# Graph sums in two one-hot steps: fixed spans of chunks first, then placed into fixed blocks

## The chip, the cores and the metric

The kernel runs on one core of a Trainium2 chip. The engines are named as in the profile: PE is TensorE (matmuls; PEld its weight loads), DVE is VectorE, ACT is ScalarE, POOL is GpSimd, and SP is SyncE, which here only issues DMAs. Times are device microseconds of one execution. The figure to be predicted is the median over several executions of the changed kernel; before the change it is 2722.78 us.

## The reference

Two graph convolutions (Chebyshev, two terms) on N = 6250 nodes with 512 features, E = 100000 edges that come sorted by their target `dst`, everything in float32:

```python
h = jnp.maximum(_layernorm(x), 0.0)
norm = -dinv[src] * dinv[dst]                 # dinv from the out-degree of each node
def prop(h):
    return segment_sum(h[src] * norm[:, None], dst, num_segments=N)
h = h @ W1_0 + prop(h) @ W1_1 + b1            # first layer
h = layer_norm(h, gamma, beta)
h = where(h >= 0, h, 0.01 * h)
out = x + h @ W2_0 + prop(h) @ W2_1 + b2      # second layer
```

For each node, `prop` adds up the rows of its incoming edges, some 16 of them. The factor `dinv[src]` is in the table from which rows are read (`tab`), the factor `-dinv[dst]` is applied to the sum.

## The kernel before, in words

**Edges and gathers.** The edges are cut into 782 chunks of 128. For each chunk POOL issues one indirect DMA (L400) that gathers the 128 source rows, 256 KB, into one of 57 places of a ring in SBUF. That makes 1564 gathers for both layers; the first 16 are issued in the prologue (L246). `gather_to` issues them up to a chunk number, and a place is free again when PE has read it.

**Sums.** A block is 128 nodes in a row, four quarters of 32. `block_plan` (L37) lays 53 blocks over a layer's nodes without looking at the data: each begins at the target of an edge whose number is fixed, so the first node of a block is known only at run time. It also says, for each quarter, which chunks may hold an edge of it, with a margin for the spread (`ranges`). `sums` makes one-hot matrices on DVE: `plain` and `node` (L503, L504) are the node numbers, `sel` (L507) compares the targets `dl` with them. In layer 0, `held` (L511) counts how many edges have been found, by which the kernel knows at the end whether any was missed. The matmuls of L517 then add up the rows: `sel` of 32 columns is the weights, the 128x512 rows of a chunk are moving, and the four quarters lie in four strips of 32 columns of the array, which work side by side. A block has six or seven such steps of up to four matmuls. ACT copies the result out of PSUM as `agg` (L520), scaled by `-dinv`.

**Products.** `transposed` (L460) turns a 128x512 tile by four PE transposes. For the own part, `h` of the block goes through it to `hT`, copied out by ACT (L488), and `start_products` (L495) multiplies it with `w0`. For the sums, `agg` goes through it, DVE copies it out as `aT` (L603), and L609 multiplies it with `w1` into the same bank `u_ps`. `finish` adds the bias; in layer 0 it does the layer norm and writes the rows of the next table and of `h_tab`, in layer 1 it adds `x` and writes `out`.

**Rows at an address in a register.** Since a block begins at a node known only at run time, all that belongs to its rows is addressed by a register of SP: `load` (L464 to L480) loads the first nodes of eight blocks into registers, then the rows of `x`, the scales of each row (`sb`, 4 bytes apiece) and, in layer 1, the rows of `h_tab`. The stores in `finish` (L529, L546, L550) go the same way.

**Order.** On PE, POOL and SP the order is that of the code (`manual_schedule`); on DVE and ACT the scheduler sets it. For block b the order on PE is: transposes of block b+1's own rows, the sums of b, half of b+1's own products, the transposes of `agg`, the other half, then the products of `aT`. The gathers up to the first chunk of b plus 57 are issued on POOL when block b begins; they come after the sums of the block before, whose places they take. In layer 0 `another` (four times a block, until 60 chunks are done) scales rows that were gathered from `x` before the first table was written.

Of the kernel before, what the change touches and what calls it, by code (L numbers as in the profile page):

```python
# [19 lines left out]
P = 128  # L20
# [5 lines left out]
NQ = P // Q  # L26
RE = 16
RAW = 60
SPREAD = 3.2
# [5 lines left out]


def block_plan(N, E):  # L37

    NC = -(-E // P)
    deg = E / N

    def sd(n):
        return math.sqrt(E * (n / N) * (1 - n / N))

    n = math.ceil((E - deg * P) / (deg * P - SPREAD * sd(P)))
    step = 16 * math.ceil((E - deg * P) / (16 * n))
    over = deg + SPREAD * math.sqrt(deg)  # L50
    res = []
    for b in range(n):
        first = b * step
        end = first + step + over if b < n - 1 else E - deg * P + SPREAD * sd(P)
        mean = first + (deg + 1) / 2 if b else 0
        res.append([(max(first, mean + deg * Q * q - SPREAD * math.hypot(sd(Q * q), deg / 3)),
                     min(end, mean + deg * Q * (q + 1) + SPREAD * math.hypot(sd(Q * (q + 1)), deg / 3)))
                    for q in range(NQ)])
    res.append([(E - deg * (P - Q * q) - SPREAD * sd(P - Q * q),
                 E - deg * (P - Q * (q + 1)) + SPREAD * sd(P - Q * (q + 1))) for q in range(NQ)])  # L60
    return step, n + 1, [[(int(lo // P), min(NC, math.ceil(hi / P))) for lo, hi in r] for r in res]


@with_exitstack
def gnn_kernel(
# [33 lines left out]


# [11 lines left out]
    step, BL, ranges = block_plan(N, E)  # L112
    NK = max(sum(hi - lo for lo, hi in r) for r in ranges)
# [12 lines left out]
    scales = dram.tile([3, NB * P], F32, name="scales")  # L126
# [7 lines left out]
    first_i = const.tile([1, BL], I32, name="first_i")  # L134
    first = const.tile([P, BL + 1], F32, name="first")
    owned = const.tile([P, BL], F32, name="owned")
    astray = const.tile([1, 1], F32, name="astray")
    signs = const.tile([P, 2], F32, name="signs")
# [5 lines left out]
    n_seen = const.tile([P, BL], F32, name="n_seen")  # L144
    sb = const.tile([P, BL, 3], F32, name="sb")
    sn = const.tile([P, BL, 2], F32, name="sn")
# [16 lines left out]
    dl_ps = ctx.enter_context(tc.tile_pool(name="dl_ps", bufs=1, space=bass.MemoryType.PSUM))  # L163
    dl = dl_ps.tile([P, NG * P], F32, name="dl")

# [3 lines left out]
    begin_i = ep.tile([1, BL + 1], I32, name="begin_i")  # L169
    begin = ep.tile([1, BL + 1], F32, name="begin")  # L170
# [4 lines left out]
    for ids, fill, name in ((src, 0, "src_c"), (dst, NO_NODE, "dst_c")):  # L175
# [11 lines left out]
        if ids is src:  # L187
            nc.sync.dma_start(src_i, src.rearrange("(p j) -> p j", j=EJ))
    nc.sync.dma_start(begin_i[:, 1 : BL - 1],
                      bass.AP(tensor=dst.tensor, offset=dst.offset + step - 1, ap=[[1, 1], [step, BL - 2]]))  # L190
# [40 lines left out]
    nc.gpsimd.memset(signs[:, 0:1], -1.0)  # L231
    nc.gpsimd.memset(signs[:, 1:2], SLOPE)
# [18 lines left out]
    all3 = ep.tile([P, 3, NB], F32, name="all3")  # L251
    rs_all, nb_all = all3[:, 0, :], all3[:, 1, :]
# [3 lines left out]
    for (i0, n), t in zip(groups, xs):  # L256
        n = min(n, NB - LAST - i0)
        for j in range(n):
            junk = ep.tile([P, D], BF, name="junk", bufs=2)
            nc.scalar.activation(junk, t[:, j, :], AF.Copy, accum_out=sums[:, i0 + j : i0 + j + 1])  # L260
        nc.scalar.activation(nm_all[:, i0 : i0 + n], sums[:, i0 : i0 + n], AF.Copy, scale=-1.0 / D)
        for j in range(n):
            junk = ep.tile([P, D], BF, name="junk", bufs=2)
            nc.scalar.activation(junk, t[:, j, :], AF.Square, bias=nm_all[:, i0 + j : i0 + j + 1],
                                 accum_out=sq_all[:, i0 + j : i0 + j + 1])
# [42 lines left out]
    with tc.tile_pool(name="fold", bufs=1) as dp, tc.tile_pool(  # L308
# [16 lines left out]
        nc.vector.tensor_copy(all3[:, 2, :], dinv)  # L325

# [12 lines left out]
    nc.vector.tensor_scalar(begin[:, 1 : BL - 1], begin_i[:, 1 : BL - 1], 1.0, float(N - P), op0=OP.add, op1=OP.min)  # L339
    nc.vector.memset(begin[:, 0:1], 0.0)  # L340
    nc.vector.memset(begin[:, BL - 1 : BL], float(N - P))
    nc.vector.memset(begin[:, BL:], float(N))
    nc.vector.tensor_copy(first_i, begin[:, :BL])
    with tc.tile_pool(name="first_ps", bufs=1, space=bass.MemoryType.PSUM) as fps:
        first_ps = fps.tile([P, BL + 1], F32, name="first_ps")
        nc.tensor.matmul(first_ps, ones[0:1, :], begin, start=True, stop=True)
        nc.vector.tensor_scalar_add(first, first_ps, 1.0)
    nc.vector.tensor_sub(owned, first[:, 1:], first[:, :BL])
    odd = ep.tile([1, 2, BL], F32, name="odd")
    nc.vector.tensor_single_scalar(odd[:, 0, :], owned[0:1, :], 0.0, op=OP.is_lt)  # L350
    nc.vector.tensor_single_scalar(odd[:, 1, :], owned[0:1, :], float(P), op=OP.is_gt)
    nc.vector.tensor_reduce(astray, odd.rearrange("o k b -> o (k b)"), AX.X, OP.add)


    with tc.tile_pool(name="turn", bufs=1) as wp:
        f = wp.tile([P, NG, P], F32, name="f")
        nc.vector.tensor_scalar_add(f, chunks[1], 1.0)
        for g in range(NG):
            nc.tensor.transpose(dl[:, g * P : (g + 1) * P], f[:, g, :], ident)
    with tc.tile_pool(name="scales_ps", bufs=1, space=bass.MemoryType.PSUM) as fps:  # L360
        all_ps = fps.tile([NB, 3, P], F32, name="all_ps")
        for k in range(3):
            nc.tensor.transpose(all_ps[:, k, :], all3[:, k, :], ident)
        all_sb = ep.tile([NB, 3, P], F32, name="all_sb")
        nc.scalar.activation(all_sb, all_ps, AF.Copy)
        nc.sync.dma_start(scales.rearrange("k (b p) -> b k p", p=P), all_sb)
# [5 lines left out]
    n_unseen = nc.values_load(unseen[0:1, 0:1], min_val=0, max_val=2 * BL,  # L372
                              skip_runtime_bounds_check_because="a count of blocks, and 1 if edges are missing")
# [5 lines left out]
def usual_path(tc, have):  # L379
    nc = tc.nc  # L380
    (x, out, tab, h_tab, scales, sidx, dl, iota_r, w_sb, W2_1, W2_0, w_late, ident, eps, ones, first_i, first, owned,
     astray, signs, sb, sn, bias1, bias2, gam, bet, n_seen, unseen, ranges, NK, N, E, D, NB, BL, NC, KD, places,
     order, groups, xs, sc, pick, src_lo, src_hi, p_id) = (
        have[n] for n in ("x out tab h_tab scales sidx dl iota_r w_sb W2_1 W2_0 w_late ident eps ones first_i first "
                          "owned astray signs sb sn bias1 bias2 gam bet n_seen unseen ranges NK N E D NB BL NC KD "
                          "places order groups xs sc pick src_lo src_hi p_id").split())
    AHEAD = 2
    R = len(order)
    with ExitStack() as es:
# [3 lines left out]
        row = {}  # L393
        is_lo, found, looked, gathered = [], 0, 0, RE

# [3 lines left out]
        def gather(layer, t):  # L399
            nc.gpsimd.indirect_dma_start(  # L400
                out=zr(t), out_offset=None, in_=x if layer == 0 and t < RAW else tab[layer],
                in_offset=bass.IndirectOffsetOnAxis(ap=sidx[:, t : t + 1], axis=0))
# [15 lines left out]
        def find(tag, bufs):  # L418
# [3 lines left out]
            ps = psum.tile([P, 4, P], F32, name=tag, bufs=bufs)  # L422
# [3 lines left out]
            is_lo.append(pool.tile([P, 4, P], F32, name="is_lo"))  # L426
# [3 lines left out]
        def look_up(tag, bufs):  # L430
# [3 lines left out]
            at_lo = psum.tile([P, 4, P], F32, name=tag, bufs=bufs)  # L434
# [18 lines left out]
        def another():  # L453
            look_up("aT_ps", 1)
            find("hT_ps", 1)

        def transposed(h, tag):
            ps = psum.tile([P, KD, P], F32, name=f"{tag}_ps", bufs=1)
            for kc in range(KD):
                nc.tensor.transpose(ps[:, kc, :], h[:, kc * P : (kc + 1) * P], ident)  # L460
            hT = pool.tile([P, KD, P], F32, name=tag, bufs=1)
            return ps, hT

        def load(layer, b):  # L464

            if b % LOADED == 0:
                n = min(LOADED, BL - b)
                _, vals = nc.values_load_multi_w_load_instructions(
                    first_i[0:1, b : b + n], engines=(SP,), min_val=0, max_val=N - P,
                    skip_runtime_bounds_check_because="held to the last block above")  # L470
                for k in range(n):
                    row[b + k] = bass.ds(vals[k], P)
            xt = pool.tile([P, D], F32, name="xt", bufs=AHEAD + 1)
# [4 lines left out]
            else:  # L478
                nc.sync.dma_start(h, h_tab[row[b], :])
            return xt, h  # L480

        def own(layer, b, xt, h):

            if layer == 0:
# [461 lines left out]
```

## Time and profile before

| what | value |
|---|---|
| three runs: median, lowest, highest | 2722.78, 2709.69, 2726.58 us |
| the profiled execution: as timed, and its span | 2729.88, 2728.0 us |
| mean clock granted to PE | 0.853 |
| gathers (L400, x1504 and x44): busy | 1422.7 and 43.8 us |
| PE's L495 products, two groups of x424: busy | 249.8 and 232.7 us |
| PE's transposes of the own rows (`hT_ps`, x424): busy | 65.8 us |
| DVE `sel` (L507, x424) and `aT` (L603, x106): busy | 122.7 and 73.3 us |
| ACT `agg` (L520, x106): busy | 72.8 us |
| DMA queues: POOL's gathers, all others; share of 16 engines | 50.2%, 12.1% |

Stages: a prologue until about 245 us (degrees, layer norm of `x`, the tables), layer 0 until about 1389, a change of layers until about 1541, in which the ring is filled again, layer 1 until 2673, and the last blocks. In the lines of groups, the columns are: line, engine, operation, output and inputs with the tile of the array, the shape and type, the number of records, then busy time and mean nanoseconds of one, then the idle time of the engine just before, with what ended most of it. A float32 matmul leaves two records, so 848 records of L609 are 424 matmuls. Waits list an engine, what waited, for what, the total in us, how often, and the longest. "remote" is a releaser that the profile cannot place among this core's engines.

### The profile page before, as it was taken

How to read it: one execution, taken by the hardware profiler on the slowest of the kernel's cores; microseconds unless marked ns; L12 is line 12 of the kernel's file. 1: busy time of each engine (PE TensorE's matmuls, PEld its weight loads, DVE VectorE, ACT ScalarE, POOL GpSimd, SP SyncE). 2: the span in 40 equal slices, each digit the busy share in tenths (PEclk: the TensorE clock that was granted, in tenths of full speed). 3: DMA queues.
4: the chain of work that ended last, by engine and by line, in shares of the span. 5: the costliest groups of instructions: out<-in, count | busy, mean ns of one | idle time of the engine just before them, and what ended most of it. 6: DMA issues, size and time to landing. Idle time of an engine off the chain costs nothing.

```text
span 2728.0 us, 23467 instructions
## 1 busy us (share of the span) xinstructions
PE 1913.8 (70%) x8137; PEld 739.4 (27%) x8137; DVE 681.2 (25%) x1422; ACT 472.9 (17%) x924; POOL 1497.2 (55%) x1579
## 2 busy tenths in 40 slices
PE   4636768777776776776684287778766687886868
PEld 4413222222222222222231122222222232222323
DVE  8823223222232232232241011111111111111111
ACT  8624212122221221221120000000000000000000
POOL 4255556556645645655525566656654656665560
PEclk9758889889887888898896688888887898897889
DMA  8565656667756655665635576766765666676661
GB/s 314 179 237 164 200 181 206 191 197 215 211 182 198 207 168 173 208 185 169 194 108 181 159 219 207 219 190 210 215 192 166 204 192 213 208 218 194 188 209 60
DMA packets 209696, 527.33 MB, mean 193 GB/s; under 512 B 51850, under 2 KB 53559, under 8 KB 209566
## 3 DMA queue, kind: packets, MB, share of 16 engines
q0 software_dynamic: 125120, 410.09, 50.2%
q1 hardware_dynamic: 84446, 115.63, 12.1%
q8 instruction: 66, 1.08, 0.2%
q14 instruction: 64, 0.52, 0.1%
HBM read 471.00 MB, written 54.60 MB: 193 GB/s over the span
## 4 chain that ended last, share of the span: by engine, by line
PE 39%; another core or an unknown queue 33%; DVE 12%; issue 11%; ACT 2%; DMA 1%; POOL 0%; SPq 0%; DVEq 0%; ACTq 0%; POOLq 0%
PE u_ps L609 17%; PE ps L517 14%; PE u_ps L495 5%; DVE sel L507 2%; DVE aT L603 1%; PE aT_ps L460 1%; PE hT_ps L460 1%; DVE u_ps L539 1%; DVE st L534 1%; DVE u_ps L531 1%; DVE lo L285 1%; DVE u_ps L541 1%; DVE hi L285 1%; DVE g L549 1%
## 5 line engine op out<-in xcount | busy, mean ns | idle before, releaser
L400 POOL DMA_INDIRECT places<-tab,sidx x1504 | 1422.7, 946 | 1079.8 <-PE ps L517 466.9
L517 PE MATMUL ps<-places,sel 128*32 128x512 f32 x4984 | 774.3, 615 | 122.8 <-issue 112.0
L517 PEld LDWEIGHTS ps<-places,sel 128*32 128x32 f32 x4984 | 194.6, 112 | 615.9 <-issue 601.0
L609 PE MATMUL u_ps<-places,aT 128*128 128x512 f32 x424 | 250.1, 744 | 143.0 <-DVE aT L603 123.4
L609 PE MATMUL u_ps<-w,aT 128*128 128x512 f32 x424 | 246.4, 735 | 121.4 <-DVE aT L603 106.4
L495 PE MATMUL u_ps<-w,hT 128*128 128x512 f32 x424 | 249.8, 720 | 107.2 <-issue 92.4
L507 DVE TENSOR_TENSOR sel<-dl,node 128x192 f32<-128x192 f32 (+3 forms) x424 | 122.7, 346 | 790.3 <-remote 511.5
L495 PE MATMUL u_ps<-places,hT 128*128 128x512 f32 x424 | 232.7, 676 | 7.3 <-issue 7.3
L488 ACT ACTIVATE hT<-hT_ps 128x512 f32<-128x512 f32 x106 | 63.2, 596 | 961.4 <-PE hT_ps L460 653.9
L520 ACT ACTIVATE agg<-ps,sn 128x512 f32<-128x512 f32 x106 | 72.8, 687 | 807.8 <-remote 502.1
L460 PE MATMUL aT_ps<-ident,agg 128*128 128x128 f32 x424 | 78.4, 315 | 173.0 <-ACT agg L520 111.4
L603 DVE COPY aT<-aT_ps 128x512 f32<-128x512 f32 x106 | 73.3, 691 | 482.3 <-remote 416.1
L609 PEld LDWEIGHTS u_ps<-places,aT 128*128 128x128 f32 x424 | 98.9, 242 | 296.7 <-DVE aT L603 153.5
L609 PEld LDWEIGHTS u_ps<-w,aT 128*128 128x128 f32 x424 | 98.4, 240 | 262.9 <-issue 136.7
L495 PEld LDWEIGHTS u_ps<-w,hT 128*128 128x128 f32 x424 | 87.3, 228 | 223.8 <-issue 200.1
L460 PEld LDWEIGHTS aT_ps<-ident,agg 128*128 128x128 f32 x424 | 57.8, 162 | 257.1 <-ACT agg L520 138.5
L495 PEld LDWEIGHTS u_ps<-places,hT 128*128 128x128 f32 x424 | 81.6, 213 | 118.8 <-issue 118.8
L527 DVE TENSOR_TENSOR u_ps<-u_ps,bias 128x512 f32<-128x512 f32 x52 | 36.4, 700 | 306.5 <-PE u_ps L609 165.8
L531 DVE TENSOR_TENSOR u_ps<-u_ps,bias 128x512 f32<-128x512 f32 x53 | 37.1, 699 | 248.1 <-PE u_ps L609 166.7
L400 POOL DMA_INDIRECT places<-in_x_dram,sidx x44 | 43.8, 996 | 82.2 <-ACT places L413 56.2
L460 PE MATMUL hT_ps<-ident,h 128*128 128x128 f32 x424 | 65.8, 279 | 30.7 <-DMA h<-h_tab 12.6
L460 PEld LDWEIGHTS hT_ps<-ident,h 128*128 128x128 f32 x424 | 53.7, 144 | 87.8 <-issue 60.5
(117 smaller groups left out, 992.5 us busy)
## 6 DMA issues: line engine op xcount, KB each, us to landing
xt<-in_x_dram SPq DMA_DIRECT2D x106, 256.0 KB
places<-tab,sidx POOLq DMA_INDIRECT x1504
tab<-t SPq DMA_DIRECT2D x53, 256.0 KB
h_tab<-g SPq DMA_DIRECT2D x53, 256.0 KB
h<-h_tab SPq DMA_DIRECT2D x53, 256.0 KB
out_dram<-t SPq DMA_DIRECT2D x53, 256.0 KB
places<-in_x_dram SPq DMA_DIRECT2D x4, 1792.0 KB
tab<-places SPq DMA_DIRECT2D x4, 1792.0 KB
```

The costliest lines, as they stand in the source:

```text
L285: nc.vector.tensor_tensor(t, s[:, g * 2 * GJ : (g + 1) * 2 * GJ].rearrange("p (j s) -> p j s", s=2)[:, :, None, :] .to_broadcast([EP, GJ, ...
L400: nc.gpsimd.indirect_dma_start(out=zr(t), out_offset=None, in_=x if layer == 0 and t < RAW else tab[layer], in_offset=bass.IndirectOffsetO ...
L460: nc.tensor.transpose(ps[:, kc, :], h[:, kc * P : (kc + 1) * P], ident)
L488: nc.scalar.activation(hT, ps, AF.Copy)
L495: nc.tensor.matmul(u_ps, hT[:, kc, :], w0[:, kc, :], start=(kc == 0), stop=False)
L507: nc.vector.tensor_tensor(sel[:, at[q] : at[q + 1], :], dl[:, lo:hi, None].to_broadcast(wide), node[:, None, q * Q : (q + 1) * Q].to_broad ...
L517: nc.tensor.matmul(ps[q * Q : (q + 1) * Q, :], sel[:, at[q] + s, :], zr(lo + s), start=(s == 0), stop=(lo + s == hi - 1))
L520: nc.scalar.activation(agg, ps, AF.Copy, scale=sn[:, b, 0:1])
L527: nc.vector.tensor_add(v, v, bias2)
L531: nc.vector.tensor_add(v, v, bias1)
L603: nc.vector.tensor_copy(aT, aT_ps)
L609: nc.tensor.matmul(u_ps, aT[:, kc, :], w1[:, kc, :], start=False, stop=(kc == KD - 1))
```

## The change

The sums no longer follow blocks. A unit is a span of 32 nodes: unit u begins at the first target of chunk 3u and takes part in the four chunks 3u to 3u+3 (`STEP`, `SPAN`). Four units make a group `g`; there are 66 groups a layer, which use four steps of four matmuls each. `first` (the first node of each unit) and `node_of` (the node that a row of a group stands for) are made in the prologue, for which the targets are now copied from PSUM to SBUF (`dlx`), and a compare and a reduce find whether the edges are sorted. The result of a group stays in SBUF as `agg[g]` (four buffers), not scaled.

The products follow 49 fixed blocks of 128 nodes. `inside[i]` lists the two or three groups that may hold nodes of block i, if a group's first node lies within 32 of where an even spread would put it. `place(i)` makes a 128x128 one-hot matrix `there` for each of these groups on DVE and multiplies `agg[g]` with it, four matmuls a group: this moves each row to its node and transposes it at once, in place of the PE transposes. DVE multiplies the result by `-dinv`, a row of 128 that SP has loaded for the block into all partitions (`to`).

All loads and stores of rows have fixed addresses now. `dense(i)` runs after the sums of the group that follows the last one of `inside[i]`. `check` tests once, in the middle of layer 0, that the edges are sorted and that the spans and the drift hold; the count of edges found goes. `hT_ps` has two banks instead of one.

The core of the diff, with lines left out:

```diff
+STEP = 3
+SPAN = STEP + 1
+DRIFT = 32
...
+        dl_ps = wps.tile([P, NG * P], F32, name="dl_ps")
         for g in range(NG):
-            nc.tensor.transpose(dl[:, g * P : (g + 1) * P], f[:, g, :], ident)
...
+            nc.tensor.transpose(dl_ps[:, g * P : (g + 1) * P], f[:, g, :], ident)
+        nc.scalar.activation(dlx[:, 1 : 1 + NC], dl_ps[:, :NC], AF.Copy)
+        down = wp.tile([P, NG, P - 1], F32, name="down")
+        nc.vector.tensor_tensor(down, f[:, :, 1:], f[:, :, : P - 1], op=OP.is_lt)
+        nc.vector.tensor_reduce(unsorted, down.rearrange("p g e -> p (g e)"), AX.X, OP.add)
...
+    GN = NQ * STEP * P * N / E
+    inside = [range(max(0, math.floor((i * P - DRIFT) / GN)), min(NS, math.ceil((i * P + r + DRIFT) / GN)))
+              for i, r in enumerate(rows)]
...
+        def load(layer, i):
+
+            own_h[i] = pool.tile([P, D], F32, name="h", bufs=AHEAD)
+            for lo, hi in parts(rows[i]):
+                nc.sync.dma_start(own_h[i][lo:hi], (h_tab if layer else x)[i * P + lo : i * P + hi, :])
+            to[i] = pool.tile([P, P], F32, name="to", bufs=AHEAD + 1)
+            nc.sync.dma_start(to[i], dup(ndinv_d[i * P : (i + 1) * P], P))
...
-            xt = pool.tile([P, D], F32, name="xt", bufs=AHEAD + 1)
-            nc.sync.dma_start(xt, x[row[b], :])
-            h = pool.tile([P, D], F32, name="h", bufs=AHEAD + 1)
-            if layer == 0:
-                nc.sync.dma_start(sb[:, b, :], scales[:, row[b]].rearrange("k p -> p k"))
-            else:
-                nc.sync.dma_start(h, h_tab[row[b], :])
...
+            for s in range(SPAN):
+                for q in range(n):
+                    if s < len(chunk[q]):
+                        nc.tensor.matmul(ps[q * Q : (q + 1) * Q, :], sel[:, q, s, :], zr(chunk[q][s]), start=(s == 0),
+                                         stop=(s == len(chunk[q]) - 1))
+            agg[g] = pool.tile([P, D], F32, name="agg", bufs=4)
+            nc.scalar.activation(agg[g][: n * Q], ps[: n * Q], AF.Copy)
+
+        def place(i, some):
+
+            r = rows[i]
+            if i not in placed:
+                placed[i] = psum.tile([P, KD, P], F32, name="aT_ps", bufs=1)
+            for g in some:
+                m = Q * min(NQ, NU - NQ * g)
+                there = pool.tile([P, P], F32, name="there", bufs=3)
+                nc.vector.tensor_scalar(there[:m, :r], iota_r[:m, :r], node_of[:m, g : g + 1], -(1.0 + i * P),
+                                        op0=OP.subtract, op1=OP.is_equal)
+                for kc in range(KD):
+                    nc.tensor.matmul(placed[i][:, kc, :r], agg[g][:m, kc * P : (kc + 1) * P], there[:m, :r],
+                                     start=(g == inside[i][0] and kc == 0),
+                                     stop=(g == inside[i][-1] and kc == KD - 1))
...
+        def dense(layer, i, u_ps, w0, w1):
...
+            if i + AHEAD < NB:
+                load(layer, i + AHEAD)
+            next_ps = None
+            if i + 1 < NB:
+                hT = own(layer, i + 1)
+            place(i, [g for g in inside[i] if i < NB - 1 or g == NS - 1])
+            aT = pool.tile([P, KD, P], F32, name="aT", bufs=1)
+            nc.vector.tensor_tensor(aT[:, :, :r], placed.pop(i)[:, :, :r],
+                                    to.pop(i)[:, None, :r].to_broadcast([P, KD, r]), op=OP.mult)
+            if i + 1 < NB:
+                next_ps = psum.tile([P, D], F32, name="u_ps")
+                products(next_ps, hT, w0, rows[i + 1], True)
+            products(u_ps, aT, w1, r, False)
+            finish(layer, i, u_ps)
+            return next_ps
...
+            for g in range(NS):
...
+                    gather_to(layer, STEP * NQ * g + R)
...
+                sums(g)
...
+                while i < NB and (inside[i].stop <= g or g == NS - 1):
+                    u_ps = dense(layer, i, u_ps, w0, w1)
+                    i += 1
                 if layer == 0:
...
+                    if g == NS // 2:
+                        check()
```

## The prediction

> **What bounds the kernel now.** I read the page first, then the windows by stage, the waits of the engines, and last the timeline of one block with gathers running and of one without.
>
> ```profile
> PE 1913.8 (70%) x8137; PEld 739.4 (27%) x8137; DVE 681.2 (25%) x1422; ACT 472.9 (17%) x924; POOL 1497.2 (55%) x1579
> PE 39%; another core or an unknown queue 33%; DVE 12%; issue 11%; ACT 2%; DMA 1%; POOL 0%; SPq 0%; DVEq 0%; ACTq 0%; POOLq 0%
> L517 PE MATMUL ps<-places,sel 128*32 128x512 f32 x4984 | 774.3, 615 | 122.8 <-issue 112.0
> L609 PE MATMUL u_ps<-places,aT 128*128 128x512 f32 x424 | 250.1, 744 | 143.0 <-DVE aT L603 123.4
> L609 PE MATMUL u_ps<-w,aT 128*128 128x512 f32 x424 | 246.4, 735 | 121.4 <-DVE aT L603 106.4
> L460 PE MATMUL aT_ps<-ident,agg 128*128 128x128 f32 x424 | 78.4, 315 | 173.0 <-ACT agg L520 111.4
> ```
>
> TensorE (PE) is the busiest engine, but it is idle 814 us of 2728. The second line is the odd one: a third of the chain is charged to a source that the profile cannot name ("remote" in the waits). The waits say who suffers:
>
> ```profile
> POOL places L400 <- PE ps L517: 466.9, 145, 19.5
> ...
> DVE aT L603 <- remote: 416.1, 57, 19.6
> ...
> ACT agg L520 <- remote: 502.1, 67, 74.6
> ```
>
> The steady windows hold 95 of the 106 blocks:
>
> ```profile
> 245.00:1389.00 1144.00, 820.35 (x3305) 303.19 (x3308) 319.93 (x702) 230.55 (x426) 649.19 (x687) 0.86 0.63 192
> ...
> 1541.00:2673.00 1132.00, 848.51 (x3475) 306.22 (x3476) 174.67 (x392) 81.81 (x145) 678.48 (x717) 0.87 0.65 201
> ```
>
> That is 2276/95 = 24.0 us per block, 18 of it PE busy. Two timelines of layer 1 show where the rest goes. First, with gathers running:
>
> ```profile
> 2014.39 1.98 PE L495 MATMUL u_ps<-places,hT 128*128 128x512 f32 x4
> ...
> 2017.73 0.69 ACT L520 ACTIVATE agg<-ps,sn 128x512 f32<-128x512 f32 x1 [7.25 <-remote]
> ...
> 2018.48 0.66 PE L460 MATMUL aT_ps<-ident,agg 128*128 128x128 f32 x4 [2.10 <-issue]
> ...
> 2026.18 0.69 DVE L603 COPY aT<-aT_ps 128x512 f32<-128x512 f32 x1 [6.90 <-remote]
> ...
> 2026.93 5.52 PE L609 MATMUL u_ps<-places,aT 128*128 128x512 f32 x8 [6.08 <-DVE aT L603]
> ```
>
> Then at the end, when no gather is left:
>
> ```profile
> 2686.69 0.30 PEld L495 LDWEIGHTS u_ps<-places,hT 128*128 128x128 f32 x2 [0.84 <-issue]
> ...
> 2689.15 0.69 DVE L603 COPY aT<-aT_ps 128x512 f32<-128x512 f32 x1 [1.12 <-PE aT_ps L460]
> ...
> 2690.66 3.60 PE L609 MATMUL u_ps<-places,aT 128*128 128x512 f32 x8
> ```
>
> In the first, the transposes are over at 2019.14 and the copy that waits for nothing else starts seven microseconds later; in the second the same copy follows the last transpose at once and PE never stops (14.1 us from block to block, L495 at 2686.69 to L495 at 2700.77). So while gathers stream, each handing-over from PE to DVE or ACT costs microseconds, and PE stands still where other work does not cover it. The kernel is bound by PE's work plus these round trips; the gathers' own issue (1564 x 1.25 us = 1955 us, 0.95 us and the 0.30 gap) is below it, and POOL waits 466.9 us for PE.
>
> **The change part by part.** All sums are against the profiled execution, span 2728.0 (2729.88 as timed). The median of the runs shown, 2722.78, is 0.3% lower.
>
> *Sums (L507 to L520).* Four column strips run side by side, so what counts is steps: 714 now (357 a layer), 774.3/714 = 1.084 us each. After: 65 groups of four steps and one of two, 262 a layer, 524 in all, 568 us. **-206.** Owing to fewer strips, node and sel ops get fewer too; they are off the path.
>
> *Place (new).* Summing the lengths of `inside` gives 130 (block, group) pairs a layer, each four f32 matmuls with 128 weight columns and 128 moving ones; an f32 matmul leaves two records, so 2080 records. Near rows: L439 (128x98, 16.5 us of 88 records and 7.1 of 32: 188 and 222 ns), the transposes of L460 (78.4/424 = 185), and a quarter of L609's record (585/4 = 146). I take 185: **+385**, bounds 304 and 462. [...]
>
> *The transposes of agg go:* **-78.** *49 blocks for 53:* the dense products are 979.0 us in four L495 and L609 rows, -73.9; the own part's transposes 65.8 us, -5.0. Together **-79.** PE's work so far: -206+385-78-79 = **+22**, a wash.
>
> *Waits.* (a) agg now has a whole group of sums between it and its reader, because block i is begun after the sums of the group that follows its last one. The 111.4 us before L460 go, except one of 54.4 us at the start of layer 1, which is the burst of gathers and stays: **-57.** (b) hT was copied while all sums ran (some 7 us). Now only place stands between the transposes and the products that need it: 2080/98 = 21 records, 3.9 us. Agg's copy began 3.3 us after the last sums record in the timeline above; with 0.6 for the copy that is just covered, on the long ones (6.9 us) it is not. Between 0 and 98 x (6.9+0.6-3.9) = 353; I take 1 us a block, nearest to the row: **+98.** (c) aT: PE is idle 264 us before L609. The cover grows from half the products (1.88 us) to all (some 3.8), which at 61 waits saves at most 116; but the signal now stands behind 21 records instead of four. With every block as bad as the one shown it is 98 x 6.08 = 596. I leave the wait of one block as it is: 264 x 98/106, **-19**, bounds -116 and +332. A late aT holds up the products, then finish, and nothing on POOL, which waits for sums alone.
>
> *Going from strips to the full array.* [...] There are 132 groups of sums instead of 106. The row shows 0.84 us before the first L495 weights after sums, against 0.24 between products: 26 x 0.6 = **+16**. [...]
>
> *The rest.* `there` is 260 DVE ops of some 206 ns (the 128x128 ident op, L235), 54 us; the scaling of aT by `to` (700 ns, as the tensor ops of L527) replaces a copy of 691. DVE is busy 25%, and the ops wait for nothing late: zero; without that cover 54 us. On SP, the scale loads and one x load a block go in layer 0, h loads take their place, and 98 `to` loads of 64 KB come: 6 MB of 527; all are issued two blocks ahead (h lands before use today, 12.6 us of PE wait in total). If they came late, each of 98 would cost part of 3 us (an x load took 2.8 us to its reader at 2682.22). The gathers wait for the sums of the group before, as now: 12 at a time, 15 us, instead of 14.75. Start: the second group's sums no longer stand behind block 0, which can take off the 19.5 and 14.2 us that POOL waited; the prologue gets a copy, a compare and a reduce (+7), the check in mid layer 0 four round trips of some 3 us (+12). Together **-5**, bounds -30 and +30. The inputs keep the usual path: group starts stray at most 18 nodes, spans hold at most 28.
>
> Sum: +22-57+98-19+16-5 = **+55**: span 2783, as timed 2785, and 0.3% less against the median: **2780 us**.
>
> **Rivals.**
> *The round trips vanish (faster).* One handing-over instead of two lies on the path of a block, and PE gets longer cover at both. If place covers hT (-98) and the products cover half of what is left before L609 (-123), the time is 2560; with all of it 2440. For it: the two-step order, and 14.1 us a block where signals are prompt. Against: the signals were 3 to 7 us late and the cover gained is 2. It decides if PE's idle time before the second products falls below some 1.2 us a block.
> *Lateness grows with PE's instructions (slower still).* At the start of layer 1, PE's records come 1.4 us apart while POOL streams, and agg waited 74.57 us. If the signal is late in proportion to the records ahead of it, (c) goes to its upper bound: 3130, half way 2960. For it: 9% more PE records. Against: the transposes alone were enough for 7 us. It decides above 3.5 us a block.
> *The gathers set the pace (nothing happens).* Stages last 1.63 us a gather (2276 us for some 1400) and the gathers stay 1564: about 2728. Against: POOL waits for PE, not the reverse.
>
> **How the numbers follow.** Likeliest case 0.45, at 2780, its own range 2690 to 2900 by the bounds of place and of the waits (0.34 slower, 0.08 same, 0.03 faster). Round trips vanish 0.27, 2440 to 2690. Lateness grows 0.18. Gathers' pace 0.10 (0.07 same, 0.03 slower). Faster 0.30, same 0.15, slower 0.55; within 1%, 27 us, a measurement of this kernel cannot tell a change from none. Leaving out a third of the faster case and the top of the slower one gives 2560 to 2930.
>
> **What would show it.** Sums 568 us; place near 385 with 2080 records; no wait for agg before it; PE idle before the products of hT near 100 and before those of aT near 245; PE busy within 40 us of before; POOL's wait for sums still hundreds of microseconds. I am wrong if place costs under 300, or if the idle time in front of aT's products moves by more than 100 either way.

## The result, and the profile after

The changed kernel takes 2886.03 us (median of four, 2850.31 to 2928.61) against 2722.01, 164 us more where the sum had +55. Ratios and their intervals leave out the slow executions, those more than 1.5% above the fastest of their kernel (two of the four here, and single ones of 4699.56 and 5697.14 us in later runs, whose cause is not known), so the ratio here, 1.053 (1.043 to 1.063), stands for 143 us. The profiled execution is the shortest of the four, with a span of 2848.5, so its trace holds +120.5.

The page after: first the busy time of the engines, then the chain of work that ended last, then PE's groups.

```profile
PE 1864.7 (65%) x8843; PEld 881.4 (31%) x8843; DVE 677.8 (24%) x1331; ACT 382.4 (13%) x715; POOL 1501.2 (53%) x1577
PE 40%; another core or an unknown queue 37%; issue 8%; DVE 7%; ACT 2%; POOL 2%; DMA 1%; POOLq 0%; SPq 0%; ACTq 0%; DVEq 0%
L478 PE MATMUL ps<-places,sel 128*32 128x512 f32 x4168 | 518.9, 608 | 55.5 <-issue 39.4
L494 PE MATMUL aT_ps<-there,agg 128*128 128x128 f32 (+2 forms) x2080 | 324.5, 292 | 196.0 <-issue 193.0
L456 PE MATMUL u_ps<-places,aT 128*128 128x512 f32 (+1 forms) x392 | 237.7, 762 | 207.5 <-DVE aT L552 204.0
L456 PE MATMUL u_ps<-w,hT 128*128 128x512 f32 (+1 forms) x392 | 256.4, 814 | 136.8 <-ACT hT L451 48.1
L456 PE MATMUL u_ps<-places,hT 128*128 128x512 f32 (+1 forms) x392 | 214.9, 699 | 164.0 <-ACT hT L451 152.6
L456 PE MATMUL u_ps<-w,aT 128*128 128x512 f32 (+1 forms) x392 | 199.2, 656 | 84.8 <-DVE aT L552 75.4
```

PE does less work than before (1864.7 against 1913.8) and stands still longer: 2848.5-1864.7 = 983.8 us against 814.2. All of the 169.6 us of added idle time is in these rows. The rows of hT's products before the change, which are not shown above, were:

```profile
L495 PE MATMUL u_ps<-w,hT 128*128 128x512 f32 x424 | 249.8, 720 | 107.2 <-issue 92.4
L495 PE MATMUL u_ps<-places,hT 128*128 128x512 f32 x424 | 232.7, 676 | 7.3 <-issue 7.3
```

In front of the products of hT it grew from 107.2+7.3 to 136.8+164.0, **+186**; in front of those of aT from 264.4 to 292.3, +28; before place, 196.0 where 173.0 stood before the transposes, +23; before the sums, 55.5 for 122.8, -67.

The loss lies in the second layer, as the windows show (columns as before; PE clock, DMA share and GB/s last):

```profile
245.00:1367.00 1122.00, 795.20 (x3625) 364.67 (x3625) 308.16 (x636) 158.78 (x278) 652.68 (x685) 0.82 0.63 195
...
1530.00:2781.00 1251.00, 790.18 (x3716) 362.30 (x3715) 178.76 (x368) 61.15 (x104) 674.82 (x711) 0.78 0.58 179
```

A group there takes 1251/(711/12) = 21.1 us. There are 66 groups for 49 blocks, so about one group in three is followed by no block: the sums of two groups then run in a row (64 records instead of 32), and their gathers come as one stream of 24 instead of 12. This is the timeline of such a place:

```profile
2002.71 7.07 PE L478 MATMUL ps<-places,sel 128*32 128x512 f32 x64
...
2009.71 0.66 PE L449 MATMUL hT_ps<-ident,h 128*128 128x128 f32 x4
...
2010.20 1.93 PE L494 MATMUL aT_ps<-there,agg 128*128 128x128 f32 x12
...
2023.26 0.37 PE L494 MATMUL aT_ps<-there,agg 128*128 128x128 f32 x1 [0.35 <-issue]
...
2032.79 0.95 POOL L380 DMA_INDIRECT places<-tab,sidx  x1 [0.30 <-issue]
2037.42 0.60 ACT L451 ACTIVATE hT<-hT_ps 128x512 f32<-128x512 f32 x1 [7.16 <-remote]
2038.07 0.50 PEld L456 LDWEIGHTS u_ps<-places,hT 128*128 128x128 f32 x2 [15.23 <-ACT hT L451]
...
2038.54 0.68 DVE L552 TENSOR_TENSOR aT<-aT_ps,to 128x512 f32<-128x512 f32 x1
```

The transposes for hT end at 2010.37, but ACT starts to copy hT at 2037.42, just after the gathers of this stream have ended (the last issue is at 2032.79; the DMA share is 0.31 from 2034 to 2038 us and 0.01 in the ten after). Twelve records of place pass in 1.9 us, then the other twelve need eleven: their starts lie 0.7 us apart or multiples of it. PE's signals go the same way. The trace has the events of its semaphore at 2012.60, 2019.72, 2022.55, 2025.37 and 2037.34 us, that is 10, 4, 4 and 17 steps of 0.705 us apart. hT's and aT's both wait for the stream to be over, and nothing covers them.

Two simple causes do not fit this place. The clock granted to PE was still 0.93 when the records slowed down, and fell to 0.50 afterwards:

```profile
2010.00:2015.00 5.00, 3.02 (x20) 2.26 (x19) 0.00 (x0) 0.00 (x0) 3.78 (x4) 0.93 0.83 278
2015.00:2020.00 5.00, 1.94 (x6) 1.39 (x7) 0.00 (x0) 0.00 (x0) 3.80 (x4) 0.50 0.73 208
```

And no packet of the instruction queues moves between 1994.5 and 2040.4 us, while PE goes on at 2038.07, so it did not wait for one of these.

The place shown is among the worst, not typical. PE's waits put down to the copy of hT are few and long:

```profile
PE u_ps L456 <- ACT hT L451: 200.7, 28, 15.6
```

Counted over layer 1, from the trace, the 15 blocks that follow two groups have 156.4 us of idle time before the products of hT, 10.4 us each. The 29 blocks that follow one group have 6.8 us, 0.2 each. For aT's products it is 62.8 and 144.0 us.

### The profile page after: what moved, and what is told of

It reads as the page before. It is cut to its first block, busy times and chain, and to the rows that moved or that the text cites. A ratio compares the mean times of both kernels' runs of the same rounds, so it can differ in the third digit from the quotient of the medians.

```text
span 2848.5 us, 23536 instructions
## 1 busy us (share of the span) xinstructions
PE 1864.7 (65%) x8843; PEld 881.4 (31%) x8843; DVE 677.8 (24%) x1331; ACT 382.4 (13%) x715; POOL 1501.2 (53%) x1577
## 3 DMA queue, kind: packets, MB, share of 16 engines
q1 hardware_dynamic: 73678, 115.36, 11.7%
## 4 chain that ended last, share of the span: by engine, by line
PE 40%; another core or an unknown queue 37%; issue 8%; DVE 7%; ACT 2%; POOL 2%; DMA 1%; POOLq 0%; SPq 0%; ACTq 0%; DVEq 0%
PE u_ps L456 23%; PE ps L478 12%; PE aT_ps L494 4%; POOL places L380 2%; DVE aT L552 1%; DVE sel L472 1%; PE hT_ps L449 1%; DMA places<-tab,sidx 1%; DVE u_ps L517 1%; DVE g L528 1%; DVE st L512 1%; DVE u_ps L509 1%; ACT agg L481 1%; DVE node L463 1%
## 5 line engine op out<-in xcount | busy, mean ns | idle before, releaser
L478 PE MATMUL ps<-places,sel 128*32 128x512 f32 x4168 | 518.9, 608 | 55.5 <-issue 39.4
L494 PE MATMUL aT_ps<-there,agg 128*128 128x128 f32 (+2 forms) x2080 | 324.5, 292 | 196.0 <-issue 193.0
L456 PE MATMUL u_ps<-places,aT 128*128 128x512 f32 (+1 forms) x392 | 237.7, 762 | 207.5 <-DVE aT L552 204.0
L494 PEld LDWEIGHTS aT_ps<-there,agg 128*128 128x128 f32 (+1 forms) x2080 | 281.7, 202 | 226.2 <-issue 222.4
L456 PE MATMUL u_ps<-w,hT 128*128 128x512 f32 (+1 forms) x392 | 256.4, 814 | 136.8 <-ACT hT L451 48.1
L456 PE MATMUL u_ps<-places,hT 128*128 128x512 f32 (+1 forms) x392 | 214.9, 699 | 164.0 <-ACT hT L451 152.6
L472 DVE TENSOR_TENSOR sel<-dlx,node 128x512 f32<-128x512 f32 x132 | 91.6, 694 | 756.3 <-remote 386.9
L456 PE MATMUL u_ps<-w,aT 128*128 128x512 f32 (+1 forms) x392 | 199.2, 656 | 84.8 <-DVE aT L552 75.4
L456 PEld LDWEIGHTS u_ps<-places,aT 128*128 128x128 f32 (+1 forms) x392 | 93.8, 249 | 347.1 <-DVE aT L552 230.1
L456 PEld LDWEIGHTS u_ps<-w,hT 128*128 128x128 f32 (+1 forms) x392 | 99.1, 266 | 262.6 <-issue 156.7
```

The lines of the kernel that those rows point to most:

```text
L456: nc.tensor.matmul(u_ps[:r], hT[:, kc, :r], w[:, kc, :], start=(start and kc == 0), stop=(not start and kc == KD - 1))
L472: nc.vector.tensor_tensor(sel[:, q : q + same, :w, :], of, node[:, q : q + same, None, :].to_broadcast([P, same, w, Q]), op=OP.is_equal)
L478: nc.tensor.matmul(ps[q * Q : (q + 1) * Q, :], sel[:, q, s, :], zr(chunk[q][s]), start=(s == 0), stop=(s == len(chunk[q]) - 1))
L494: nc.tensor.matmul(placed[i][:, kc, :r], agg[g][:m, kc * P : (kc + 1) * P], there[:m, :r], start=(g == inside[i][0] and kc == 0), stop=(g ...
```

## The experiments

The runs of one group share a chip, and the groups fell on different chips: there the kernel before itself took 2725, 2624, 2093, 2089 and 2707 us. So every ratio is to the runs of the kernel before on the same chip, and the third and fourth groups are read apart. Each chip was used for one group only, so a chip and the time at which it was used cannot be told apart. In these groups the changed kernel itself was run in the fourth alone; where its 1.053 is set beside a ratio below, that is the first measurement, not one of the same group.

The theories: **A**, while gathers stream back to back, PE's signals and records come out slowly and what is due waits for the end of the stream (**A1**: by the number of PE's records; **A2**: by time alone). **B**, the prediction's: each handing-over has a fixed price. **C**: the price is that of starting a stream. **H**: it counts where in the cycle the handings-over stand.

### Gathers spaced, the own part earlier, no gathers

```diff
 (in gather_to, after each gather, in both kernels)
+                nc.gpsimd.memset(spare, 0.0)        # spare: 128 x 128
```

> The changed kernel with one small POOL memset (128x128, some 0.2 us) after each gather, so that gathers come every 1.45 us instead of 1.25. Theory A (while gathers stream back to back, what PE reports goes out at one per 0.71 us, so PE stands still until the stream is over): the spare seventh lets the reports pass, PE's idle time before the products falls, 2550 to 2750 us. Theory B (each handing-over costs a fixed time that has nothing to do with the density of the stream): streams only get longer, 12 x 0.2 = 2.4 us a group of 21, 2850 to 3150 us.

> The kernel before with the same memset after each gather. Theory A: below 2650 us, with fewer remote waits. Theory B: 2720 to 3000 us.

Measured 2656.78 us, 0.981 of the kernel before (0.976 to 0.985), and 2524.31, 0.935 (0.924 to 0.945). Gathers then start every 1.34 us, not 1.45 as expected. Theory A: both kernels get faster by putting more work on the busy POOL. In the spaced kernel before, the waits for aT are almost gone (264.4 before):

```profile
L611 PE MATMUL u_ps<-places,aT 128*128 128x512 f32 x424 | 205.9, 631 | 11.9 <-issue 8.4 <-DVE aT L605 3.5
L611 PE MATMUL u_ps<-w,aT 128*128 128x512 f32 x424 | 200.7, 618 | 24.1 <-DVE aT L605 19.6 <-issue 4.5
```

The two kernels stay as far apart as without the memset (0.981/0.935 = 1.049).

```diff
-                hT = own(layer, i + 1)              # in dense, after the sums
...
+                    early[i + 1] = own(layer, i + 1)   # before sums(g), where dense(i) follows
```

> The changed kernel with the own part's transposes of the next block back in front of the sums, as in the kernel before, so that hT is copied while the sums run. Theory A (reports held back by the stream): PE's wait for hT goes (some 200 us), but the wait for aT takes most of it over, since both signals leave only when the stream is over: 2820 to 2900 us. Theory B (two separate round trips, each of a fixed price): the wait for hT goes and nothing comes in its place, 2620 to 2720 us.

2734, 2755 and 2844 us beside 2725, with no interval (the fourth execution is the one of 5697 us): between the two theories. The first two are on average 119 us below the 2850.31 and 2876.06 us of the changed kernel, so by them this one move takes back most of the loss of 143 us; the third does not show it. The idle time before the products of hT fell from 301 to 109 us in its trace, but that before place (190) and aT's products (303) did not.

```diff
-                    gather_to(layer, STEP * NQ * g + R)
+                    gather_to(layer, min(STEP * NQ * g, NC if layer == 0 else 0) + R)
```

> The changed kernel with layer 1 gathering only the first 57 chunks; the other chunks of layer 1 are left out and the rows that lie in the ring are summed in their place. Theory A: without a stream layer 1 runs at PE's own pace, some 11 us a group, 720 us in place of 1400, about 2150 to 2200 us in all. Theory B: the round trips stay at 3 us or more each, 17 us a group, 2500 us in all.

2309.51 us, in one execution, above what A said; the last gather of layer 0 ended at 1444 us instead of 1367. But where no gather is left, PE does not stop once (window lines of layer 1):

```profile
1700.00:1900.00 200.00, 200.00 (x1147) 96.27 (x1150) 54.92 (x114) 18.68 (x32) 0.00 (x0) 1.00 0.18 57
1900.00:2100.00 200.00, 200.00 (x1150) 96.89 (x1143) 56.12 (x115) 19.14 (x32) 0.00 (x0) 1.00 0.19 60
```

Four groups take 43.7 us there (starts of their sums), 10.9 a group, not 21.1. The handing-over has no fixed price; B falls.

### Records, placings, streams

```diff
-                nc.tensor.matmul(u_ps, hT[:, kc, :], w0[:, kc, :], start=(kc == 0), stop=False)
+                for n in range(2):
+                    cut = slice(n * D // 2, (n + 1) * D // 2)
+                    nc.tensor.matmul(u_ps[:, cut], hT[:, kc, :], w0[:, kc, cut], start=(kc == 0 and n == 0), stop=False)
```

> The kernel before with each matmul of the own part's products cut into two of 256 columns: 16 more records of PE in a block (8 matmuls, 8 weight loads), with the same columns streamed. Theory A1 (while gathers stream, what counts is how many records PE issues beyond the first 100 or so): up to 16 x 0.71 = 11 us a block, 150 to 600 us more. Theory A2 (after some 8 us of stream all of PE's reports are late, however many records there are) and theory B (fixed round trips): 0 to 50 us more.

2860.57 us, 1.089 (1.078 to 1.100) for the same columns. In the last blocks, with no gathers, the sums start 14.1 and 13.7 us apart; without the split it was 14.1 and 13.6. So records cost nothing of their own, and some 236 us where gathers stream. Half of the added ones stand in front of the signal of the transposes of agg, the other half just behind it, and the products after that signal are where the time is:

```profile
L611 PE MATMUL u_ps<-places,aT 128*128 128x512 f32 x424 | 278.9, 818 | 247.8 <-DVE aT L605 188.0 <-issue 59.8
L611 PE MATMUL u_ps<-w,aT 128*128 128x512 f32 x424 | 253.8, 754 | 189.7 <-DVE aT L605 188.4 <-issue 1.3
```

437.5 us of idle time before aT's products, 264.4 without the split in the trace of the first measurement. A2 falls, since 0 to 50 us were its forecast: the number of records counts.

```diff
 (with lines left out)
-            place(i, [g for g in inside[i] if i < NB - 1 or g == NS - 1])
+            place(i, [inside[i][-1]])
```

> The changed kernel with each block placed from the last of its groups alone: 49 instead of 130 placings a layer, so 1296 matmul records fewer; the nodes of the other groups are left out. Their own time is 1296 x 0.156 = 202 us. Theory A1: they cost more than that, since their weight loads and matmuls are also the records that PE is short of: 300 to 600 us less than the changed kernel. Theory A2 and B: at most the 202 us, more likely half of it, 2680 to 2800 us.

2622.21 us, 0.997 (0.991 to 1.002): 5.6 points below the changed kernel's 1.053, some 150 us. That is less than A1 said and within the 202 us of A2 and B, so this run does not speak for A1. With fewer records ahead of aT's signal the idle time before its products went to 109 us, but hT's rose:

```profile
L456 PE MATMUL u_ps<-w,hT 128*128 128x512 f32 (+1 forms) x392 | 263.4, 834 | 340.2 <-ACT hT L451 138.5 <-issue 132.2 <-DVE aT L552 56.5
L456 PE MATMUL u_ps<-places,hT 128*128 128x512 f32 (+1 forms) x392 | 242.9, 777 | 191.5 <-ACT hT L451 182.9 <-issue 8.3
```

532 us before hT's products, whose signal stands behind all the sums and has now less work to cover it. That the missing cover moved the time there is a reading of these rows; no run tests it alone.

```diff
-                else:
+                elif g % 2 == 0 or (layer == 0 and g < 12):
                     gather_to(layer, STEP * NQ * g + R)
```

> The changed kernel with the gathers issued for two groups at a time, 24 in one stream, so that a stream starts 33 times a layer instead of 66. Theory C (each start of a stream costs some 6 us, and the changed kernel has 66 for 53): 200 to 400 us less. Theory A: a longer stream holds PE back for longer, between 0 and 150 us more.

2849.2 us, 1.088 (1.078 to 1.098). The edit did less than was meant: POOL's gathers keep their order, and each still starts when its own place is free. In layer 1 of this trace there are 25 streams of 12 gathers and 15 of 22 to 24, and in the changed kernel 26 and 15; only in layer 0 the long ones went from 4 to 13. So this run hardly tests C or a longer stream, and the 3.5 points above the changed kernel's 1.053 may be the chip's. C falls by the two traces that were there before: in layer 1 the changed kernel has 47 streams (a new one after every pause of POOL over 1.5 us) and the kernel before 52, and it is the changed kernel that takes longer there, 1251 against 1132 us.

> The changed kernel with both: the own part's transposes before the sums, and a POOL memset after each gather. Theory A: with prompt signals the order matters less, so within 60 us of the spaced kernel without it (2657), 2590 to 2680 us. Theory B: the same 90 us or so come off as without the spacing, 2540 to 2590 us. If the change's own PE work decided (it is a few per cent less than before), it would come under the 2524 of the kernel before with the memset.

2584.47 us, 0.984 (0.974 to 0.994), the same as the spaced kernel without it (0.981), as A said. In microseconds it lies in B's range, but both ranges were written for the first chip, on which the kernel before takes 100 us more, so the ratio is read. In this trace 230 us of idle time remain before aT's products: the spacing helps the changed kernel less than the kernel before.

### Both handings-over in front of the sums

```diff
 (dense is cut in two; the first half runs before sums(g) where dense(i) follows it)
+        def front(layer, i):
+            ...
+            hT = own(layer, i + 1) if i + 1 < NB else None
+            place(i, [g for g in inside[i] if i < NB - 1 or g == NS - 1])
+            aT = pool.tile([P, KD, P], F32, name="aT", bufs=1)
+            nc.vector.tensor_tensor(aT[:, :, :r], ...)
+            return hT, aT
...
+                if g < NS - 1 and inside[i].stop <= g:
+                    ready[i] = front(layer, i)
                 sums(g)
```

> The changed kernel with the transposes of the next block's own part, place and the scaling of aT all moved in front of the sums of the group (their inputs are there by then), so that after the sums only products follow, and both handings-over are covered by the sums. Theory H (the loss is where the handings-over stand in the cycle): PE's waits for hT and aT, 480 us, go nearly all, 0.90 to 0.97 of the kernel before. Theory A1 (PE gets a limited number of records out while gathers stream, wherever the waits are): the idle time turns up elsewhere on PE, 1.00 to 1.06.

> The same with a POOL memset of 128x128 after each gather. Theory H: 0.86 to 0.93 of the kernel before. Theory A1: about what the spaced changed kernel reached, 0.95 to 0.99.

> The changed kernel with each block placed from the last of its groups alone (the nodes of the others are left out), and the own part's transposes before the sums. Placing one group alone gave 0.997 with 321 us of waiting for hT. Theory A1: with that wait gone the 1296 matmul records show their full price (0.28 us a record pair in the kernel with the split products), 0.90 to 0.95. Theory B: only the fixed round trip goes, 0.96 to 0.98.

> The kernel before with a memset twice as wide, so that gathers come every 1.44 us instead of 1.34. Theory A: PE's waits shrink further, but the gathers' own pace (14.75 x 1.44 = 21.2 us a block) is now what a block takes: 0.93 to 0.96 of the kernel before, no better than with the shorter memset.

This group fell on a chip on which nothing of this can show, because the signals are prompt (with both handings-over in front PE stands idle 1.4 us before aT's products): 1.024 (1.022 to 1.025), 1.093 (1.092 to 1.095), 1.020 (1.019 to 1.022) and 1.153 (1.151 to 1.155) of a kernel before that takes 2093 us. The memset that helped on the first chip costs here; what PE waits for is the gathers' own pace (243.0 us for gathers to land in the first). The fourth group, on another such chip (2089 us), has the changed kernel itself:

> The changed kernel itself, beside the three below on one chip. On a chip where the signals come late (as in the first two groups of runs) 1.04 to 1.06 of the kernel before, as measured. On a chip where they are prompt (as in the third group, where the kernel before took 2093 us and the gathers' pace ends it) both kernels should be near the gathers' 1955 us: 1.00 to 1.04.

> The changed kernel with transposes, place and scaling moved in front of the sums. On a chip with late signals, theory H (where the handings-over stand): 0.90 to 0.97; theory A1 (a limited number of PE records while gathers stream): 1.00 to 1.06. On a chip with prompt signals 1.02 as measured, within 0.01 of the changed kernel.

> The changed kernel with only the own part's transposes moved in front of the sums. On a chip with late signals 1.01 to 1.04 (three of the four earlier executions gave 2734, 2755 and 2844 us beside 2725). On a chip with prompt signals within 0.01 of the changed kernel.

> As the run before, with each block placed from the last of its groups alone (the nodes of the others are left out). On a chip with late signals, theory A1: 0.90 to 0.95, since the wait for hT no longer takes over what the missing records set free; theory B: 0.96 to 0.98. On a chip with prompt signals 1.02 as measured.

1.022 (1.020 to 1.025), 1.026 (1.023 to 1.028), 1.022 (1.020 to 1.024) and 1.022 (1.020 to 1.024): neither order nor fewer placings matter. The changed kernel's groups there:

```profile
L478 PE MATMUL ps<-places,sel 128*32 128x512 f32 x4168 | 715.2, 668 | 254.9 <-DMA places<-tab,sidx 249.8 <-DVE sel L472 2.0
L494 PE MATMUL aT_ps<-there,agg 128*128 128x128 f32 (+2 forms) x2080 | 248.8, 275 | 1.4 <-ACT agg L481 1.4
L456 PE MATMUL u_ps<-places,hT 128*128 128x512 f32 (+1 forms) x392 | 178.4, 598 | 0.7 <-ACT hT L451 0.7
L456 PE MATMUL u_ps<-places,aT 128*128 128x512 f32 (+1 forms) x392 | 176.3, 592 | 0.7 <-DVE aT L552 0.7
```

PE waits only for gathers to land. Between the ends of a layer POOL has no gap over 1.5 us. So the 49 us on such a chip lie where no gathers run. In the changed kernel's waits of POOL:

```profile
POOL places L380 <- ACT places L394: 70.0, 2, 69.7
POOL places L380 <- DMA tab<-t: 33.6, 1, 33.6
```

and in those of the kernel before with the wider memset, the only trace of the older design from such a chip:

```profile
POOL places L401 <- ACT places L414: 57.5, 2, 57.4
POOL places L401 <- DMA tab<-t: 21.9, 1, 21.9
```

12.5 us more at the start and 11.7 at the change of layers; two shorter gaps of POOL in the prologue (11.5 and 6.7 us against 6.5 and 5.1) add 6.6; after the last gather 30.5 us to the end against 17.7, 12.8 more. That is some 44 of 49; the rest is open. The last of these figures is the least sure, since with gathers further apart PE can have less left to do after the last one. The last group fell on a chip with late signals again:

> The kernel before, unchanged, for its trace on this chip. On a chip with prompt signals: some 2090 us, POOL issuing its gathers with no waits for PE, and, against the changed kernel on such a chip, a shorter gap of POOL at the start, at the change of layers and after the last gather, 47 us in all. On a chip with late signals: 2620 to 2740 us, as before.

> The changed kernel with transposes, place and scaling moved in front of the sums, once more, for a chip with late signals. There, theory H (where the handings-over stand) gives 0.90 to 0.97 of the kernel before, theory A1 (a limited number of PE records while gathers stream) 1.00 to 1.06. On a chip with prompt signals 1.02, as measured twice.

The first took 2717.36 us, as on the first chip. The second took **2531.15 us, 0.938 (0.931 to 0.944)**: theory H. With the same instructions in another order the changed kernel goes from 1.053 (first measurement) to 0.938, and the waits for hT and aT are gone (groups of that run):

```profile
L479 PE MATMUL ps<-places,sel 128*32 128x512 f32 x4168 | 744.2, 650 | 173.2 <-issue 148.1
L457 PE MATMUL u_ps<-w,hT 128*128 128x512 f32 (+1 forms) x392 | 229.9, 723 | 100.4 <-issue 48.1 <-DVE g L529 41.3 <-ACT hT L452 8.5
L457 PE MATMUL u_ps<-places,hT 128*128 128x512 f32 (+1 forms) x392 | 186.4, 619 | 1.3 <-ACT hT L452 0.7 <-issue 0.4
L457 PE MATMUL u_ps<-w,aT 128*128 128x512 f32 (+1 forms) x392 | 177.6, 593 | 4.7 <-issue 3.8 <-DVE aT L551 0.7
L457 PE MATMUL u_ps<-places,aT 128*128 128x512 f32 (+1 forms) x392 | 176.3, 592 | 0.7 <-DVE aT L551 0.7
L495 PE MATMUL aT_ps<-there,agg 128*128 128x128 f32 (+2 forms) x2080 | 309.4, 296 | 169.0 <-issue 133.9 <-ACT agg L482 34.8
```

107 us before all the products, 593 in the changed kernel as it was. Not all of these 486 us came off the time: the sums' records, whose number is the same, kept PE busy for 744.2 us instead of 518.9, so part of it did turn up elsewhere on PE, as A1 had it. PE's slow records remain (169 before place, 173 before the sums) but nothing is behind them that the next step waits for. No version beats the kernel before everywhere: this one is 2 to 3% slower on the two chips with prompt signals.

## Why the prediction was right and wrong

Right were the direction, that PE's own work is a wash (+22 foreseen, -49 found), and that waits for signals decide. The time lies in the stated range, but the loss of the trace is twice the +55, and that hides larger misses of both signs: +88 at hT, +80 at agg and place, +47 at aT, -83 before the sums, -71 in PE's work, and 5 for the ends. By its steps:

- *Sums, place, products.* Sums went from 774.3 to 518.9 (-255, foreseen -206). There was luck in this: the same records kept PE busy for 744.2 us in the order with both handings-over in front, and for 715.2 where signals are prompt. Place took 324.5 us (385), 156 ns a record; the rows' 185 was too much. Where signals are prompt it was 248.8/2080 = 120 ns. Products fell by 71 (74).
- *Wait (a), agg:* -57 foreseen. The wait for agg did go (1.4 us), but PE stood still 196 us before place, on its own slow records: +23 by those rows. Not foreseen.
- *Wait (b), hT: the step that failed.* "I take 1 us a block, nearest to the row: +98." It is +186. The row was agg's copy, 3.3 us behind the last record of the sums. For the blocks that follow one group this price was not too low (0.2 us each in layer 1). It failed at the 15 of 44 blocks there that follow two groups, with 10.4 us each. The prediction had the gathers come "12 at a time, 15 us"; behind two groups 24 come in one stream. The own part's transposes had moved behind the sums' records in that stream, so their signal left when it ended, 27 us later in the place shown. Whether the longer stream or the 32 more records of the sums count there, no run separates. The bound 353 held. The sign "near 100" left out the 114.5 us that stood before these products already; by the sum it would have been near 212, and 301 was found.
- *Wait (c), aT:* -19 foreseen (-20 by its own working), +28 found; the longer cover and the records ahead of the signal nearly cancel. In the split kernel, with 16 more records a block, the wait was 173 us longer than in the trace of before, so the lateness of the second rival, which grows with the records, was seen there; it was set against fixed prices and given too little weight.
- *Going from strips to the full array:* no run shows the +16. The idle time before the sums fell by 67 us, and in the stretch with no gathers PE is busy for 200.00 of 200.00 us though sums and products take turns there: the 0.84 us before the weights was no idle time of PE there.
- *Ends of the layers:* -5 foreseen; where the gathers' pace is all, some 44 us of loss lie there.

Neither of the two signs of being wrong came (place 324.5, aT +28): none had been set on hT. The faster rival was a matter of order, not of the two-step sums: with both handings-over in front of the sums its time came (0.938, 2560 foreseen).

Open remains what the slow signals are and why chips differ in it. Every execution here left records of its instructions, so it is not known whether PE would be as late if none were written. Open too is what placing one group alone brings with hT early where signals are late, since that fell on prompt chips both times.

## What to carry to other kernels

Where a stream of gathers makes signals late, as on three of five chips here, ask of each handing-over how many of the producer's records precede its signal since the stream began (here 437.5 us of idle time before aT's products with the split, 264.4 without) and what work lies between it and its reader. Look for the places where two steps run in a row and their transfers join into one stream: the average step does not show them (here 10.4 us of idle time a block behind two groups, 0.2 behind one). Issue producers early, in front of the long work that needs none of them (0.938 here, where the changed kernel as it was had 1.053 in the first measurement), and don't price a moved wait by the row it had in its old place. Compare on more than one chip before a pause in the stream, or an order, is called faster: with both handings-over in front the changed kernel took 0.938 of the kernel before on one chip, 1.024 and 1.026 on two others.

## What the runs showed of the hardware

The kernel before took between 2089 and 2725 us on five chips (medians), within 3.3% on each. On three of them PE stood idle for hundreds of microseconds before aT's products: 303.2 us with hT early (chip of the first group), 437.5 us with the split (second), 257.0 us in the kernel before (fifth). In the place shown, from the first measurement, in a stream of back-to-back gathers (210 GB/s, DMA share 0.74), PE's records came 0.7 us apart or multiples of it, from 8.5 us after the start of the stream; its signals followed the same step. On the two other chips the idle time before aT's products was 1.4 us in the changed kernel (with both handings-over in front on the third, as it was on the fourth), and on the fourth 782 gathers of one layer took 986 us, 1.26 us each. On the first group's chip, 0.09 us more between the starts of gathers (1.34 for 1.25 us) took 6.5% off the kernel before; on the third's, 1.44 us put 15% on.
